# A recommender on one core: part of the history fetched as columns of an item table held in SBUF

## The chip, the core and the metric

The kernel runs on one core of a Trainium2 chip. The metric is the device time of one execution in microseconds (us). A core has five engines with queues of their own: PE (TensorE, matrix products), DVE (VectorE), ACT (ScalarE), POOL (GpSimd) and SP (SyncE, which here only issues transfers). On-chip memory is SBUF, with 128 partitions, and PSUM, which PE writes.

## The reference

There are 50,001 items and 16,384 users. An item has 32 neighbours. For two embeddings of 32 numbers (in and out) an attention of each item over its neighbours gives two vectors of 32. With a history embedding of 64 this makes an item row of 128; with a target embedding of 64, and the two vectors swapped, a target row of 128. Each user has a history of 100 items and one target.

```python
V = E[near_full]
scores = jnp.einsum('nd,nkd->nk', E, V) / jnp.sqrt(jnp.float32(GEO_HALF))
w = jax.nn.softmax(scores, axis=-1)
attn_of_item = jnp.einsum('nk,nkd->nd', w, V)
...
x = h * t[:, None, :]                      # h: [users, 100, 128], t: [users, 128]
z = jax.nn.relu(jnp.einsum('bld,hd->blh', x, W1) + b1)
scores = jnp.einsum('blh,h->bl', z, W2[0])
mask = (history != target[:, None]) & (history != 0)
exp_A = jnp.exp(scores) * mask
attn = exp_A / (jnp.sum(exp_A, axis=-1) ** 0.5)[:, None]
s = jnp.sum(h * attn[..., None])           # one number over everything
```

The result is the sigmoid of a cosine between the target row and a vector that has the number s in all places. So of each history row two things are needed: its score, and the plain sum of its 128 numbers. All data is float32.

## The kernel before

The kernel has two stages, one after the other, and a short end.

**Item stage.** Items go in 391 tiles of 128, each with 32 neighbours to fetch. POOL fetches most with one indirect gather of 128 rows per neighbour (line 238). The others come from `geoT`, the embedding table held transposed in SBUF: an item is a column there, and ACT and DVE copy one column of four bytes at a time (line 258), or PE copies it as a one-column product with the identity (line 253). A column's address stands in a register, and 32 registers are loaded at a time (line 197). SP fetches some neighbours row by row (line 226). The attention is worked out on DVE and ACT. `finish` (line 374) writes the rows to the tables `table` and `ttab` in DRAM.

**User stage.** Users go in 128 blocks of 128, and a block's 100 history positions in groups of 8 (the last of 4). For a group:

- `gather` (line 561) lets POOL fetch 8 rows per user with 8 indirect gathers (line 572), into one of six buffers.
- `turn` (line 581) transposes the 8 tiles on PE (line 587), multiplies them on DVE by the transposed target (line 589), and sums each row on DVE (line 592).
- `hidden` (line 601), one group later, multiplies by W1 on PE, 512 columns at a time (line 607), and applies Relu on ACT (line 608).
- `scored` (line 611), two groups later, multiplies each position by w2, a one-column product (line 616).

Each float32 product is two passes in the trace, a transpose one. `one_by_one` (line 534) has SP fetch some groups row by row, one transfer for each of 128 x 16 rows (line 555). `target_rows` and `target_work` fetch and transpose the target's rows, one gather per block (line 501). In the item stage the order of the engines' work is written out by hand; in the user stage it is the planner's, in the main over the loop at line 637.

Of the kernel before, what the change touches and what calls it, by code (L numbers as in the profile page):

```python
# [18 lines left out]
P = 128  # L19
ITEMS = 50001  # L20
K = 32
G = 32
# [32 lines left out]
BSUB = 4  # L55
LG = 4
NG = L // LG

UG = 2
UNIT = 42  # L60
AHEAD = 4
# [3 lines left out]
def kernel(  # L65
# [18 lines left out]
    geoT = nc.alloc_sbuf_tensor("geoT", (P, PAIRS), F32).ap()  # L84
# [3 lines left out]
    const = ctx.enter_context(tc.tile_pool(name="const", bufs=1))  # L88
    dram = ctx.enter_context(tc.tile_pool(name="dram", bufs=1, space=bass.MemoryType.DRAM))


    table = dram.tile([ROWS, D], F32, name="table")

    ttab = dram.tile([ROWS, D], F32, name="ttab")

    ident = const.tile([P, P], F32, name="ident")
    make_identity(nc, ident)
    ones = const.tile([P, P], F32, name="ones")
    nc.vector.memset(ones, 1.0)
    b1_sb = const.tile([HID, 1], F32, name="b1_sb")  # L100
    nc.sync.dma_start(b1_sb, b1.rearrange("(h o) -> h o", o=1))
    w2_sb = const.tile([HID, 1], F32, name="w2_sb")
    nc.sync.dma_start(w2_sb, w2.rearrange("o h -> h o"))
    w1_sb = const.tile([HID, D], F32, name="w1_sb")
    nc.sync.dma_start(w1_sb, w1)
    w1T = const.tile([D, HID], F32, name="w1T")
    with tc.tile_pool(name="wps", bufs=1, space=bass.MemoryType.PSUM) as wps:
        w1_ps = wps.tile([D, HID], F32, name="w1_ps")
        nc.tensor.transpose(w1_ps, w1_sb, ident)
        nc.vector.tensor_copy(w1T, w1_ps)  # L110
# [12 lines left out]
    with (  # L123
# [15 lines left out]
        def load(it):  # L139
# [5 lines left out]
            row = n_in.tile([P, NSUB, D + G], F32, name="row")  # L145
            nc.sync.dma_start(row[:, :, 0:DE], ehist_v[it])
# [216 lines left out]
        def attended(s):  # L363
            it, j = divmod(s, NSUB)
            row = its[it][2]
            att, tot = subs[s]["att"], subs[s]["ex"][1]
            nc.vector.tensor_tensor(
                row[:, j, DE:D].rearrange("p (t d) -> p t d", t=2),
                att,
                tot.to_broadcast([P, 2, G]),  # L370
                ALU.mult,
            )

        def finish(s):
            it, j = divmod(s, NSUB)
            row = its[it][2]
            nc.scalar.copy(row[:, j, D : D + G], row[:, j, DE : DE + G])

            if j == NSUB - 1 or (it == NITER - 1 and j == NSUB - 2):
                j0 = NSUB - 1 if it == NITER - 1 and j == NSUB - 1 else 0  # L380
                js = slice(j0, j + 1)
                nc.scalar.dma_start(ttab_v[it][:, js, DE:D], row[:, js, DE + G : D + G])
                nc.scalar.dma_start(table_v[it][:, js, :], row[:, js, 0:D])
# [75 lines left out]
    num = const.tile([P, UC], F32, name="num")  # L459
    den = const.tile([P, UC], F32, name="den")  # L460
    tsum = const.tile([P, UC], F32, name="tsum")
    tsq = const.tile([P, UC], F32, name="tsq")
    hist_v = history.rearrange("(p i j) l -> i p j l", p=P, j=BSUB)
    tidx = const.tile([P, UC], I32, name="tidx")
    nc.scalar.dma_start(tidx, target.rearrange("(p c) -> p c", p=P))
    tidf = const.tile([P, UC], F32, name="tidf")
    nc.vector.tensor_copy(tidf, tidx)
    with (
        tc.tile_pool(name="u_in", bufs=AHEAD + 2) as u_in,
        tc.tile_pool(name="u_t", bufs=2) as u_t,  # L470
        tc.tile_pool(name="u_h", bufs=6) as u_h,
        tc.tile_pool(name="u_hs", bufs=2) as u_hs,
        tc.tile_pool(name="u_x", bufs=2) as u_x,
        tc.tile_pool(name="u_s", bufs=2) as u_s,
        tc.tile_pool(name="ps_t", bufs=2, space=bass.MemoryType.PSUM) as ps_t,
        tc.tile_pool(name="ps_z", bufs=2, space=bass.MemoryType.PSUM) as ps_z,
        tc.tile_pool(name="ps_s", bufs=2, space=bass.MemoryType.PSUM) as ps_s,
    ):
        users = {}
        hists = {}  # L480
        LW = 2 * LG
        NW = -(-L // LW)
        in_order = mybir.DependencyInfo(
            mybir.DependencyClass.NoSync, mybir.DependencyReason.DATA
        )

        def width(g):
            return min(LW, L - g * LW)

        table_b = table.bitcast(U8).rearrange("(o r) d -> o (r d)", o=1)  # L490

        def history_of(i):
            hidx = u_in.tile([P, BSUB, L], I32, name="hidx")
            tc.keep_in_program_order(nc.sync.dma_start(hidx, hist_v[i]))
            hists[i] = hidx

        def target_rows(c):


            t = u_t.tile([P, D], F32, name="t")  # L500
            nc.gpsimd.indirect_dma_start(
                out=t,
                out_offset=None,
                in_=ttab[0:ITEMS, :],
                in_offset=bass.IndirectOffsetOnAxis(ap=tidx[:, c : c + 1], axis=0),
            )
            users[c] = {"t": t, "hidx": hists[c // BSUB][:, c % BSUB, :]}

        def target_work(c):
            u = users[c]  # L510
            t = u["t"]
            tT_ps = ps_t.tile([P, LG, P], F32, name="hT_ps")
            nc.tensor.transpose(tT_ps[:, 0, :], t, ident)
            tT = u_t.tile([D, 1, P], F32, name="tT")
            nc.vector.tensor_copy(tT[:, 0, :], tT_ps[:, 0, :])
            u["tT"] = tT
            nc.vector.tensor_reduce(tsum[:, c : c + 1], t, AX.X, ALU.add)
            junk = u_t.tile([P, D], F32, name="junk")
            nc.scalar.activation(junk, t, AF.Square, accum_out=tsq[:, c : c + 1])
            idf = u_s.tile([P, L], F32, name="idf")  # L520
            nc.scalar.copy(idf, u["hidx"])
            keep = u_s.tile([P, L], F32, name="keep")
            nc.vector.tensor_scalar(keep, idf, 0.0, None, ALU.not_equal)
            nc.vector.scalar_tensor_tensor(
                keep, idf, tidf[:, c : c + 1], keep, ALU.not_equal, ALU.mult
            )
            u["keep"] = keep
            u["hsum"] = u_s.tile([P, L], F32, name="hsum")
            u["score"] = ps_s.tile([P, L], F32, name="score")
            u["xT"], u["z"] = {}, {}  # L530

        early = {}

        def one_by_one(c, g):

            hs = u_hs.tile([P, UG * LW, D], F32, name="hs")

            hoff = u_hs.tile([P, UG * LW], I32, name="hoff")
            nc.vector.tensor_scalar(
                hoff,  # L540
                hists[c // BSUB][:, c % BSUB, g * LW : (g + UG) * LW],
                9,
                None,
                ALU.logical_shift_left,
            )
            for p in range(P):
                _, vals = nc.values_load_multi_w_load_instructions(
                    hoff[p : p + 1, :],
                    engines=[E.SP],
                    min_val=0,  # L550
                    max_val=(ITEMS - 1) * 4 * D,
                    skip_runtime_bounds_check_because="worked out from an item's number",
                )
                for q in range(UG * LW):
                    nc.sync.dma_start(
                        hs[p : p + 1, q, :].bitcast(U8), table_b[:, ds(vals[q], 4 * D)]
                    )
            for i in range(UG):
                early[c, g + i] = hs[:, i * LW : (i + 1) * LW, :]

        def gather(c, g):
            u = users[c]
            if (c, g) in early:
                u["h", g] = early.pop((c, g))
                u["got", g] = []
                return
            h = u_h.tile([P, LW, D], F32, name="h")
            u["got", g] = []
            for q in range(width(g)):
                l = g * LW + q  # L570
                u["got", g].append(
                    nc.gpsimd.indirect_dma_start(  # L572
                        out=h[:, q, :],
                        out_offset=None,
                        in_=table,
                        in_offset=bass.IndirectOffsetOnAxis(ap=u["hidx"][:, l : l + 1], axis=0),
                    )
                )
            u["h", g] = h

        def turn(c, g):
            u = users[c]
            w = width(g)
            h = u.pop(("h", g))
            hT_ps = ps_t.tile([P, LW, P], F32, name="hT_ps")
            for q in range(w):
                nc.tensor.transpose(hT_ps[:, q, :], h[:, q, :], ident)  # L587
            xT = u_x.tile([D, LW, P], F32, name="xT")
            x = nc.vector.tensor_tensor(  # L589
                xT[:, 0:w, :], hT_ps[:, 0:w, :], u["tT"].to_broadcast([D, w, P]), ALU.mult  # L590
            )
            s = nc.vector.tensor_reduce(  # L592
                u["hsum"][:, g * LW : g * LW + w], h[:, 0:w, :], AX.X, ALU.add
            )
# [147 lines left out]
```

## Time and profile before

| | us |
|---|---|
| median of three runs (29,659.82 to 29,660.97) | 29,659.96 |
| span of the profiled execution | 29,732.2 |
| POOL busy | 22,274.0 (75%) |
| PE busy | 20,868.1 (70%) |
| DVE busy | 14,649.3 (49%) |
| ACT busy | 10,176.0 (34%) |

The profile is of one execution, with its own time, a little longer than the median. Its lines give the source line, engine, operation and tiles (written from read), how often, the busy time, the mean duration of one in ns, and the idle time before them with what ended it. An idle time that ends with "issue" waited for nothing that the profile shows. Durations of one can overlap, so a pace is read from starts. The row PEclk gives the granted share of PE's clock in tenths, in 40 slices of the span; the other rows there are busy tenths. The clock is granted in windows of 3.41 us, at half or full rate in this trace.

### The profile page before, as it was taken

The page shows a single profiled execution, that of the slowest core. Times are in us where ns is not written, and L with a number is a line of the kernel's source. Part 1 is how long each engine was busy: PE and PEld are TensorE (multiplying, and loading weights), DVE is VectorE, ACT ScalarE, POOL GpSimd, SP SyncE. Part 2 cuts the span into 40 slices and gives each one's busy share as a digit, 9 for nine tenths or more (in the row PEclk, how much of TensorE's full clock was granted, in tenths as well). Part 3 has the DMA queues.
Part 4 walks back from the last instruction along what each step waited for, and adds up shares of the span by engine and source line. Part 5 has one row for each costly group of instructions (what it writes and reads, how often), then busy time and mean ns, then how long its engine had stood idle before and what let it go on. Part 6 is the DMA issues. An engine that isn't in the chain of part 4 may idle for free. (4 is left out here: it accounts for less than half of the span.)

```text
span 29732.2 us, 544828 instructions
## 1 busy us (share of the span) xinstructions
PE 20868.1 (70%) x85960; PEld 15598.5 (52%) x85960; DVE 14649.3 (49%) x92225; ACT 10176.0 (34%) x80592; POOL 22274.0 (75%) x23541
## 2 busy tenths in 40 slices
PE   5666666666666666667777777777777777777777
PEld 4666666666666666665444444444444444444444
DVE  5787777777877777774222222222222222222222
ACT  4555555555555555552111111111111111111111
POOL 7777777777777777777777777777777777777777
PEclk9999999999999999997666666666666666666666
DMA  3111111111111111112222222222222222222222
GB/s 68 34 33 33 35 34 32 33 35 34 33 33 35 34 33 33 35 33 47 53 54 54 54 54 54 54 54 54 54 54 54 54 54 54 54 54 54 54 54 52
DMA packets 1112201, 1351.31 MB, mean 45 GB/s; under 512 B 626480, under 2 KB 726256, under 8 KB 1108704
## 3 DMA queue, kind: packets, MB, share of 16 engines
q0 software_dynamic: 753120, 1186.89, 17.8%
q1 hardware_dynamic: 204528, 78.25, 1.0%
q10 hardware_dynamic: 151056, 51.31, 0.7%
q14 instruction: 2738, 22.43, 0.3%
q8 instruction: 759, 12.44, 0.2%
HBM read 1276.16 MB, written 51.30 MB: 45 GB/s over the span
## 5 line engine op out<-in xcount | busy, mean ns | idle before, releaser
L572 POOL DMA_INDIRECT h<-table,hidx x12512 | 11836.9, 946 | 3831.0 <-issue 3500.9
L238 POOL DMA_INDIRECT v<-in_egeo_dram,nidx x10895 | 10315.4, 947 | 3331.8 <-issue 3205.2
L253 PE MATMUL pc<-geoT,ident 128*128 x39424 | 8444.3, 352 | 312.5 <-issue 312.5
L253 PEld LDWEIGHTS pc<-geoT,ident 128*128 128x128 f32 x39424 | 8438.2, 333 | 392.9 <-issue 392.6
L258 ACT COPY g<-geoT 128x4 uint8 x73920 | 7265.1, 189 | 3174.6 <-issue 2704.0
L258 DVE COPY g<-geoT 128x4 uint8 x83776 | 6536.7, 196 | 1097.4 <-issue 1092.3
L589 DVE TENSOR_TENSOR xT<-hT_ps,tT 128x1024 f32<-128x1024 f32 (+1 forms) x1664 | 1969.0, 1183 | 10043.1 <-PE hT_ps L587 10043.1
L587 PE MATMUL hT_ps<-ident,h 128*128 128x128 f32 x12512 | 4502.9, 391 | 3162.9 <-DMA h<-table,hidx 3005.9
L608 ACT ACTIVATE z<-z_ps,b_sb 128x512 f32<-128x512 f32 x3200 | 2199.0, 687 | 11904.4 <-PE z_ps L607 11900.4
L587 PEld LDWEIGHTS hT_ps<-ident,h 128*128 128x128 f32 x12512 | 2177.1, 180 | 7692.6 <-DMA h<-table,hidx 6903.2
L607 PE MATMUL z_ps<-xT,w1T 128*128 128x512 f32 x6400 | 5585.9, 980 | 476.3 <-DVE xT L589 476.1
L616 PEld LDWEIGHTS score<-w_sb,z 128*128 128x128 f32 x25600 | 3759.7, 224 | 188.5 <-issue 167.7
L616 PE MATMUL score<-w_sb,z 128*128 128x1 f32 x25600 | 3494.9, 259 | 0.0
L281 PE MATMUL pt<-ident,g 128*128 128x128 f32 x1386 | 414.6, 435 | 4112.4 <-DVE g L258 3591.1
L281 PEld LDWEIGHTS pt<-ident,g 128*128 128x128 f32 x1386 | 270.5, 233 | 4185.4 <-issue 3220.7
L607 PEld LDWEIGHTS z_ps<-xT,w1T 128*128 128x128 f32 x6400 | 1810.9, 337 | 737.5 <-DVE xT L589 505.7
L592 DVE TENSOR_REDUCE hsum<-h 128x8 f32<-128x1024 f32 (+1 forms) x1628 | 1900.1, 1167 | 0.0
L307 DVE TENSOR_TENSOR prod<-v,own_ps 128x2048 f32<-128x2048 f32 x391 | 894.5, 2288 | 1340.0 <-DMA v<-in_egeo_dram 661.7
L347 DVE TENSOR_TENSOR wv<-v,ex 128x1024 f32<-128x1024 f32 x782 | 1473.8, 1886 | 0.0
L317 DVE TENSOR_REDUCE sc<-prod 128x64 f32<-128x2048 f32 x391 | 889.5, 2275 | 0.2
L360 DVE TENSOR_REDUCE att<-wv 128x64 f32<-128x2048 f32 x391 | 883.5, 2260 | 0.2
L289 ACT COPY v<-pt 128x256 f32<-128x256 f32 (+1 forms) x385 | 135.1, 351 | 1624.6 <-PE pt L281 1604.5
(74 smaller groups left out, 2045.9 us busy)
## 6 DMA issues: line engine op xcount, KB each, us to landing
hs<-table SPq DMA_DIRECT2D x36864, 0.5 KB
v<-in_egeo_dram SPq DMA_DIRECT2D x29568, 0.2 KB
h<-table,hidx POOLq DMA_INDIRECT x12512
v<-in_egeo_dram,nidx POOLq DMA_INDIRECT x10895
table<-row ACTq DMA_DIRECT2D x22, 1088.0 KB
own<-in_egeo_dram SPq DMA_DIRECT2D x23, 544.0 KB
row<-in_ehist_dram SPq DMA_DIRECT2D x23, 544.0 KB
ttab<-in_etgt_dram ACTq DMA_DIRECT2D x1, 12500.0 KB
```

What stands on the lines that cost most here:

```text
L238: nc.gpsimd.indirect_dma_start(out=v[:, k].rearrange("p t d -> p (t d)"), out_offset=None, in_=egeo, in_offset=bass.IndirectOffsetOnAxis(a ...
L253: nc.tensor.matmul(g[:, i : i + 1], ident, column.bitcast(F32), start=True, stop=True)
L258: copy(g.bitcast(U8)[:, 4 * i : 4 * i + 4], column)
L307: nc.vector.tensor_tensor(prod.rearrange("p k t d -> p k (t d)"), v.rearrange("p k t d -> p k (t d)"), subs[s]["own"].to_broadcast([P, K, ...
L347: nc.vector.tensor_tensor(subs[s]["wv"][:, t].rearrange("p d k -> p k d"), subs[s]["v"][:, :, t, :], subs[s]["ex"][0][:, t, :] .rearrange( ...
L572: nc.gpsimd.indirect_dma_start(out=h[:, q, :], out_offset=None, in_=table, in_offset=bass.IndirectOffsetOnAxis(ap=u["hidx"][:, l : l + 1], ...
L587: nc.tensor.transpose(hT_ps[:, q, :], h[:, q, :], ident)
L589: x = nc.vector.tensor_tensor(xT[:, 0:w, :], hT_ps[:, 0:w, :], u["tT"].to_broadcast([D, w, P]), ALU.mult)
L592: s = nc.vector.tensor_reduce(u["hsum"][:, g * LW : g * LW + w], h[:, 0:w, :], AX.X, ALU.add)
L607: nc.tensor.matmul(z_ps, w1T, xT[:, q : q + LG, :], start=True, stop=True)
L608: nc.scalar.activation(z[:, q : q + LG, :], z_ps, AF.Relu, bias=b1_sb)
L616: nc.tensor.matmul(u["score"][:, l : l + 1], z[:, q, :], w2_sb, start=True, stop=True)
```

## The change

The item stage stays, but for the row that it writes: `table` has rows of 129 numbers, the sum of the row first. The user stage is new.

- A stage between the two gives back `geoT`'s memory and loads the whole of `table` again, in 196 parts, to hold it transposed in SBUF as `tab` (128 x 50,001). The same loop fetches all target rows, 128 gathers, and stores them transposed in DRAM as `tgtT`.
- Of a block's 100 positions 88 are rows as before, in 30 groups of 3 (two of them of 2), in six row buffers of one tile each. SP fetches three rows in two blocks row by row, at the groups in `BY_SP`.
- The other 12 positions are six pairs. ACT copies the first of a pair, DVE the second, as 128 columns each out of `tab`, 25 or 26 in a group (`CHUNK`), over five groups a pair. The last nine of each (`EARLY`) are put off to the next group, ahead of its load of registers. The addresses are worked out once per block (`addresses`), in group 12 of the block before.
- PE takes a row's sum with a one-column product of the identity and the stored sum, and a pair's sums with a one-column product of the columns and a vector of ones.
- The order of all five engines is now written out by hand. In PE's: the sums of a pair if one is complete, the first row, the hidden product of the group before (and of a pair), the second row, the scores of the group two before (and of a pair), the third row.

```diff
+W = 1 + D
+GR = 3
+SIZES = ([3] * 14 + [2]) * 2
+NGR = len(SIZES)
+NROW = sum(SIZES)
+PAIRED = (L - NROW) // 2
+TURN = NGR // PAIRED
+CHUNK = (26, 26, 26, 25, 25)
+EARLY = 9
+BY_SP = (19, 39, 58)
+NRING = 6
+CH = 2
...
+                nc.vector.tensor_reduce(row[:, js, 0], row[:, js, 1:W], AX.X, ALU.add)
...
+    geoT_held.__exit__(None, None, None)
+    tc.strict_bb_all_engine_barrier()
+    tab_held = nc.sbuf_tensor("tab", (D, ITEMS), F32)
...
+            def turned(q):
...
+                nc.sync.dma_start(
+                    st[0:h, 0:n, :],
+                    table[base : base + h * n, 1:W].rearrange("(p n) d -> p n d", n=n),
+                )
+                ps = hidden_tile()
+                for r in range(n):
+                    nc.tensor.transpose(ps[:, r, 0:h], st[0:h, r, :], ident[0:h, 0:h])
+                into = tab[:, base : base + h * n].rearrange("d (p n) -> d n p", n=n)
+                copy = nc.vector.tensor_copy if q % 3 == 2 else nc.scalar.copy
+                copy(into, ps[:, 0:n, 0:h])
...
+            def addresses(c):
...
+                nc.tensor.transpose(cols_ps[0:n, :], colf[:, 0:n], ident)
+                nc.vector.tensor_copy(cols[r0:n, :], cols_ps[r0:n, :])
...
+            def turn(s, q):
+                c, g = divmod(s, NGR)
+                l = firsts[g] + q
+                h = rows[s][q]
+                nc.tensor.transpose(hT[s][:, q, :], h[:, 1:W], ident)
+                nc.tensor.matmul(sums[c][:, 1, l : l + 1], ident, h[:, 0:1], start=True, stop=True)
...
+            def columns(s, engine, of, early):
...
+                for i in range(n - EARLY, n) if early else range(n - EARLY):
+                    copy(
+                        into[:, 4 * (i0 + i) : 4 * (i0 + i) + 4],
+                        tab_b[:, ds(vals[i] - tab_at, 4)],
+                    )
...
+                if pairs[0]:
+                    pc, k = pairs[0]
+                    for i in range(2):
+                        l = NROW + 2 * k + i
+                        nc.tensor.matmul(
+                            sums[pc][:, 1, l : l + 1],
+                            pair[at[0] * TURN][:, i, :],
+                            unit,
+                            start=True,
+                            stop=True,
+                        )
+                for q in range(GR):
+                    if s < last and q < SIZES[g]:
+                        turn(s, q)
+                    if q == 0 and 1 <= s <= last:
+                        hidden(s - 1)
+                        relu(s - 1)
+                        if pairs[1]:
+                            x = pair[at[1] * TURN]
+                            zp = hidden_tile()[:, 0:2, :]
+                            nc.tensor.matmul(zp, w1T, x, start=True, stop=True)
+                            nc.scalar.activation(x, zp, AF.Relu, bias=b1_sb)
+                    if q == 1:
+                        if 2 <= s < last + 2:
+                            scored(s - 2)
+                        if pairs[2]:
+                            pc, k = pairs[2]
+                            for i in range(2):
+                                score(pc, NROW + 2 * k + i, pair[at[2] * TURN][:, i, :])
+                if s < last:
+                    times_target(s)
...
+                for engine, of in ((E.Activation, 0), (E.DVE, 1)):
+                    columns(s, engine, of, True)
+                    columns(s, engine, of, False)
```

## The prediction

> **What bounds the kernel now.** I read the page's slices first: they split the run into two stages.
>
> ```profile
> PE   5666666666666666667777777777777777777777
> ACT  4555555555555555552111111111111111111111
> POOL 7777777777777777777777777777777777777777
> PEclk9999999999999999997666666666666666666666
> L572 POOL DMA_INDIRECT h<-table,hidx x12512 | 11836.9, 946 | 3831.0 <-issue 3500.9
> ```
>
> POOL is level over both stages. Its 12,512 user gathers take (11,836.9 + 3,831.0) / 12,512 = 1.252 us each, and nearly all the idle time is the engine's own issuing: POOL bounds. One line's own view gives the stage's ends.
>
> ```profile
> L572 POOL DMA_INDIRECT h<-table,hidx x12512: 943/947/1038, 13673.8 to 29713.5; - x199
> ```
>
> The first target gather stands at 13,671 in the timeline, so the user stage is 29,732 - 13,671 = 16,061 us: 125.5 us for each of 128 user blocks. SP's rows come every 0.324 us beside it. PE is second, 11,986 us busy of 16,061, at a mean granted clock of 0.66. Since the change gives PE more work, I look at PE's pace in a stretch recorded at half clock (13,747 to 13,802 us), then in the item stage.
>
> ```profile
> 13749.18 1.91 PE L607 MATMUL z_ps<-xT,w1T 128*128 128x512 f32 x2
> 13750.89 0.93 PE L587 MATMUL hT_ps<-ident,h 128*128 128x128 f32 x2
> ...
> 13754.05 0.48 PE L587 MATMUL hT_ps<-ident,h 128*128 128x128 f32 x1 [0.32 <-DMA h<-table,hidx]
> 13754.32 1.71 PE L616 MATMUL score<-w_sb,z 128*128 128x1 f32 x8
> 13755.89 0.45 PE L587 MATMUL hT_ps<-ident,h 128*128 128x128 f32 x1
> ...
> 13576.81 27.46 PE L253 MATMUL pc<-geoT,ident 128*128 x128 [1.31 <-issue]
> ```
>
> Starts, not durations, give the pace. The hidden product of 512 columns takes 13750.89 - 13749.18 = 1.71 us (two passes), so 0.427 for a position of 128 columns. One-column products take 27.46 / 128 = 0.2145 us a pass, two passes each: 0.429. A transpose with eight such passes takes 13755.89 - 13754.05 = 1.84 us; less six passes (1.29), a transpose with one two-pass product is 0.55. All these halve at full clock (there a one-column pass takes 0.112 us). The clock row reads 9 in the item stage, but line 253 keeps the half-clock pace there, and the first gate record of the trace is at 13,693 us: those nines are no reading.
>
> When the gate opens is seen by cutting the stage at the gate's own 3.41 us windows, for the hidden products alone (columns: PE, weight loads, ACT, granted clock, DMA).
>
> ```profile
> 20004.11:20007.52 3.41, 0.25 (x1) 0.51 (x2) 0.00 (x0) 0.50 0.21 54
> 20007.52:20010.94 3.42, 2.79 (x4) 0.69 (x3) 0.69 (x1) 0.50 0.18 44
> 20010.94:20014.35 3.41, 0.46 (x1) 0.00 (x0) 0.69 (x1) 1.00 0.22 61
> 20014.35:20017.76 3.41, 0.38 (x1) 0.60 (x2) 0.00 (x0) 0.50 0.25 59
> 20017.76:20021.18 3.42, 2.94 (x4) 0.60 (x2) 0.69 (x1) 0.50 0.19 48
> 20021.18:20024.59 3.41, 0.32 (x1) 0.00 (x0) 0.69 (x1) 1.00 0.18 50
> ```
>
> A window at full clock follows one filled with hidden products: a group of 8 sends four passes in a row. I counted streaming time (transposes 0.213, hidden products by columns; one-column passes as nothing) in all 3,155 half-clock windows of the stage: under 2.4 us the next was never at full clock, over 2.7 always. Windows with 16 one-column passes closed the gate again.
>
> **The change, step by step.** *Item stage*: the row gains a sum (one DVE reduction per 17 tiles, near 2.3 us as line 360's) and 4 bytes; POOL still sets the pace. 13,671 us stay.
>
> *New stage between*: 196 loads of 128 KB turn the table, with 128 target gathers (128 x 1.25 = 160 us, beside it). Nearest row: the 66 loads of `st` between 55 and 181 us, 1.9 us each with three transposes, among other work. Bounds 200 us (1 us a load) and 450 us; SP's tgtT store waits each of 43 times for the step's end with the next loads behind it, so I take 350.
>
> *POOL, per user block*: 88 rows less 1.5 by SP = 86.5 x 1.252 = 108.3 us. Alone that is 17 us a block, 2,200 us in all, saved.
>
> *ACT*: 768 columns at 95 ns (32 in 3.14 us) are 73 us. Each of 30 loads of registers takes, scaled from 1.98 us for 32, 1.6 us for 25.6; the nine columns kept back hide 0.86, leaving 30 x 0.75 = 23. Thirty Relus near 0.52 (0.69 for 512) and the rest: 20. Sum 116 us. *DVE*: 768 x 0.071 + 30 x 1.15 + 30 x 0.58 + 4 = 110. *SP*: 192 x 0.324 + 6 x 2.2 = 75. All within 125.5. That line 592's reductions go (1,900 us of DVE) is worth nothing by itself: DVE was idle three quarters of the stage.
>
> *PE* at half clock: a row was 0.213 + 0.427 + 0.429 = 1.07 us, 107 us a block, inside 125.5. The row sum moves from DVE to PE: each row has one more one-column product with the identity as weights, two passes. A row is 0.55 + 0.427 + 0.429 = 1.41; 88 make 123.7. A position fetched as a column still needs sum, hidden product and score: 1.285 x 12 = 15.4. Together 139.1.
>
> PE also gains waits. (a) Once per five groups it sums a pair by column, first in the group's order, and waits for DVE's last nine columns, which DVE runs only after the product with the target: 0.25 (end of transpose) + 0.06 + 0.58 + 0.64 less the 0.43 that PE still has = 1.1 us, six times 6.6. (b) In group 12 the transpose of the addresses waits for a DVE queue of product, columns and five small operations: 0.2 + 0.58 + 3 + 0.9 less 0.3 = 4.4 us. Behind PE wait the transposes of rows already landed, and behind those the gathers, with six row buffers. Together 150.1 us a block, over POOL's 108: PE becomes the bound unless the gate opens.
>
> *Does it?* By the Trainium skill (TensorE: Matmul & The Clock Gate, Part 1) some 3.4 us of sustained matmul activity opens the gate and only idle closes it. PE without pauses would then be at full clock: 70 + 11 us, ACT the bound at 117 with its waits on PE, and the sum 13,671 + 350 + 128 x 117 + 20 = 29,017. The row of line 253 says otherwise: 27 us without a pause at half pace; streamed columns count, not weight loads. The groups of 3 now spread the hidden products: an ordinary window holds at most 3 x 0.213 + 1.28 = 1.92 us. Only a pair's group (0.85 more) can reach 3.23 us of dense work with 2.56 streamed, 2.7 with the next transpose, if the free-running window falls on it within a few tenths of a us. I allow one open window of six such groups: it does 6.8 us of half-clock work in 3.4. So 150.1 - 3.4 = 146.7 us a block. (The same page, Part 4, says that transposes don't count as busy; I count them, which favours the change.)
>
> *Sum*: 13,671 + 350 + 128 x 146.7 (18,778) + 20 for the end = 32,819 us in the profiled execution. The median of the runs is 29,660 to the profile's 29,732, 0.24% less: 32,740. I say 32,750, 10.4% slower.
>
> **Rivals.**
> - *The gate opens* (0.14, the other side): the place is PE's pace per block, the price 139 / (1 + share at full clock) + 11. With before's user stage plus the new one the break-even is (16,061 - 350) / 128 = 122.7 us, a share of 0.25; above it ACT's 117 soon binds, so 29,017, on the runs' scale 28,950. For: before had a share of 0.32 (clock 0.66). Against: it came from four passes in a row, which the change splits, and a gate opened here starves PE (six landed rows), so it closes again.
> - *The gate opens at times* (0.13): shares of 0.08 to 0.22 give 140 to 125 us, 30,000 to 31,900. For: a pair's group lies close to the threshold, and the period of five groups may lock to the window.
> - *The gate stays shut and more waits come* (0.05): each us a block is 128 us. Scores wait for ACT, a row of SP for its 128 transfers (near 50 us of the 100 there are). Over 33,900.
> - *POOL stays the bound and PE's work is hidden* (within the first): 108.3 a block would give 27,900; it needs ACT faster too.
>
> **How the numbers follow.** The main case has 0.68, its own range 32,100 (two open windows a block) to 33,250 (none, 150.1). To leave out no more than 2 in 10, the range goes down through most of the second rival and up past the new stage's bound: 30,800 to 34,000. Faster by over 0.2%, which is about what a measurement of this kernel can tell: 0.14. Within 0.2%: 0.02, where the share happens to be 0.25. Slower: 0.84.
>
> **What would show it.** Right: in the user stage POOL's idle time goes to waits for PE (the one-column sum that frees a row), PE is busy nearly throughout, the clock row near 0.5, rows every 1.6 us. PE's waits in that stage are for DVE's columns (six a block) and addresses (one, 4 us). Wrong: a clock row of 7 or more with POOL gathers still 1.25 us apart; or one-column passes with the identity under 0.2 us at half clock; or the new stage outside 200 to 450 us.

## The result, and the profile after

The changed kernel takes 39,965.43 us (median of four runs, 39,964.99 to 39,966.9) against 29,659.89 us before: 1.3475 times as long, with a 95% interval of 1.3456 to 1.3494. The forecast was 32,750 us, at most 34,000. The direction was right and the size was not.

First the slices of the changed kernel's page, which answer to the four rows shown of before.

```profile
PE   5666666666666577777777777777777777777777
ACT  4565565555555444444444444444444444444444
POOL 7777777777777544444444444444444444444443
PEclk9999999999999999555555555555555555555555
```

POOL is no longer level: in the user stage it falls from 7 to 4 tenths. The clock row settles at 5, as predicted. But PE, which was to be "busy nearly throughout", stands at 7, and ACT falls to 4. Nothing is full: something else is waited for.

The stage is cut into its parts next (the changed kernel; the columns are the length, then PE, weight loads, DVE, ACT and POOL busy, the granted clock, the DMA share and GB/s).

```profile
0.00:13650.00 13650.00, 8881.20 (x41030) 8703.85 (x41030) 10728.77 (x87867) 7862.11 (x76872) 10286.56 (x10901) 1.00 0.16 35
13650.00:14038.00 388.00, 149.98 (x517) 84.01 (x517) 104.87 (x274) 81.69 (x257) 120.67 (x128) 1.00 0.40 110
14038.00:39924.00 25886.00, 18560.79 (x71739) 15477.03 (x71740) 10091.51 (x104152) 11985.09 (x103189) 10436.36 (x11072) 0.54 0.12 30
```

The item stage ends at 13,650 us and the new stage takes 388. The whole loss lies in the user stage: 25,886 us from the first gather of history rows to the last, 202.2 us a block, where 125.5 were before and 146.7 forecast. PE is busy for 18,561 / 128 = 145.0 us of a block, so it waits 57.2.

Who waits for whom is in the changed kernel's waits (sum in us, times, longest) and in two of its groups.

```profile
POOL h L643 <- PE sums L656: 14370.7, 8391, 6.9
DVE pair L713 <- issue: 12321.8, 3888, 5.2
ACT pair L713 <- issue: 10150.6, 3835, 4.6
PE z L676 <- DVE xz L665: 4041.7, 1416, 4.5
...
PE sums L755 <- DVE pair L713: 1833.6, 767, 3.4
...
PE hT L604 <- DVE colf L601: 825.9, 128, 7.3
...
PE sums L755 <- ACT pair L713: 620.8, 646, 1.6
```

```profile
L643 POOL DMA_INDIRECT h<-table,hidx x11072 | 10437.3, 943 | 15449.7 <-PE sums L656 14370.7
L713 ACT COPY pair<-tab 128x4 uint8 x98304 | 10067.1, 190 | 10172.4 <-issue 10163.3
L713 DVE COPY pair<-tab 128x4 uint8 x98304 | 8100.6, 184 | 12349.0 <-issue 12337.0
```

POOL waits for the row sum that frees a row, as predicted (14,371 us). PE's four waits add up to 7,322 us, which is 57.2 us a block, all of what it isn't busy. All four are for what DVE or ACT owes. DVE and ACT in turn stand before their columns for 96 and 79 us a block "for issue": for nothing but their own queue. What the queue holds there is the load of registers, which isn't counted as busy. Its line shows it (minimum, median and maximum in ns): line 197 of the kernel before, which the forecast scaled from, then line 609 of the changed kernel.

```profile
L197 DVEq TENSOR_LOAD <-cols x2618: 2097/2152/6565, 221.2 to 13634.2; - x187
L197 ACTq TENSOR_LOAD <-cols x2310: 1937/1982/6642, 215.8 to 13626.7; - x193
```

```profile
L609 ACTq TENSOR_LOAD <-cols x3840: 1917/5372/5644, 14042.1 to 39939.3; - x192
L609 DVEq TENSOR_LOAD <-cols x3840: 2065/5589/5926, 14044.7 to 39942.5; - x192
L609 SPq TENSOR_LOAD <-cols x768: 2080/2174/2337, 14042.1 to 39844.7; - x192
```

A load of 25 or 26 registers takes 5.4 us at the median, where one of 32 took 1.98 before. The minimum of 1.92 says that some are still short. DVE's timeline in the changed kernel shows which:

```profile
20001.78 0.56 DVE L665 TENSOR_TENSOR xz<-hT,tT 128x384 f32<-128x384 f32 x1 [4.59 <-PE hT L655]
20002.25 0.86 DVE L713 COPY pair<-tab 128x4 uint8 x9
20007.76 1.24 DVE L713 COPY pair<-tab 128x4 uint8 x16 [4.65 <-issue]
20008.91 0.42 DVE L665 TENSOR_TENSOR xz<-hT,tT 128x256 f32<-128x256 f32 x1
...
20029.40 0.72 DVE L713 COPY pair<-tab 128x4 uint8 x9
20031.08 1.35 DVE L713 COPY pair<-tab 128x4 uint8 x17 [0.95 <-issue]
```

After the nine columns that were kept back comes the load, and then 16 or 17 columns. The gap is 4.65 us at one place and 0.95 at another. DVE's product with the target (line 665) stands behind it, PE's hidden product behind that, POOL's gather behind PE. Sorted by the five parts of `CHUNK`, the loads fall in two classes. `cols` holds four bytes a number:

| part | first byte | registers | ACT, us | DVE, us |
|---|---|---|---|---|
| 1 | 0 | 26 | 1.95 | 2.08 |
| 2 | 104 | 26 | 5.61 | 5.82 |
| 3 | 208 | 26 | 1.95 | 2.08 |
| 4 | 312 | 25 | 5.40 | 5.60 |
| 5 | 412 | 25 | 5.40 | 5.60 |

(Medians of 768 loads each; within a part they differ by at most 0.24 us.) The short ones start at a multiple of 16 bytes, the long ones don't, and those take 0.216 us a register on ACT. Three of five loads are long. (SP's loads of 32 all start at multiples of 128 bytes, and at 2.17 us they are as short as before.) The theory is that the start of the read, not the number of registers, is the cause. The rivals: PE's own work at half clock would have cost as much without the long loads; or a load is long for where it stands between columns, not for its address.

### The profile page after: what moved, and what is told of

Same layout as the page of the kernel before. It is cut to its first block, busy times and chain, and to the rows that moved or that the text cites. A ratio compares the mean times of both kernels' runs of the same rounds, so it can differ in the third digit from the quotient of the medians.

```text
span 39964.1 us, 799690 instructions
## 1 busy us (share of the span) xinstructions
PE 27610.5 (69%) x113357; PEld 24280.8 (61%) x113357; DVE 20940.0 (52%) x192415; ACT 19945.1 (50%) x180432; POOL 20844.5 (52%) x22101
## 5 line engine op out<-in xcount | busy, mean ns | idle before, releaser
L713 ACT COPY pair<-tab 128x4 uint8 x98304 | 10067.1, 190 | 10172.4 <-issue 10163.3
L713 DVE COPY pair<-tab 128x4 uint8 x98304 | 8100.6, 184 | 12349.0 <-issue 12337.0
L676 PE MATMUL z<-xz,w1T 128*128 128x384 f32 (+1 forms) x7680 | 6178.6, 908 | 4047.9 <-DVE xz L665 4047.9
L656 PEld LDWEIGHTS sums<-h,ident 128*128 128x128 f32 x22144 | 6162.8, 344 | 1355.1 <-issue 1355.0
L685 PE MATMUL sums<-small,xz 128*128 128x1 f32 x22528 | 5293.0, 350 | 0.0
L685 PEld LDWEIGHTS sums<-small,xz 128*128 128x128 f32 x22528 | 5218.7, 330 | 0.2
L655 PE MATMUL hT<-ident,h 128*128 128x128 f32 x11072 | 4874.2, 440 | 1.8 <-DMA h<-table,hidx 1.8
L656 PE MATMUL sums<-h,ident 128*128 128x1 f32 x22144 | 4686.9, 281 | 0.0
L655 PEld LDWEIGHTS hT<-ident,h 128*128 128x128 f32 x11072 | 3515.2, 317 | 952.0 <-issue 854.8
L680 ACT ACTIVATE xz<-z,small 128x384 f32<-128x384 f32 (+1 forms) x3840 | 2182.7, 568 | 3738.5 <-PE z L676 3696.6
```

What stands on the lines that cost most here:

```text
L655: nc.tensor.transpose(hT[s][:, q, :], h[:, 1:W], ident)
L656: nc.tensor.matmul(sums[c][:, 1, l : l + 1], ident, h[:, 0:1], start=True, stop=True)
L676: nc.tensor.matmul(z[s][:, 0:w, :], w1T, xz[s][:, 0:w, :], start=True, stop=True)
L680: nc.scalar.activation(xz[s][:, 0:w, :], z.pop(s)[:, 0:w, :], AF.Relu, bias=b1_sb)
L685: nc.tensor.matmul(sums[c][:, 0, l : l + 1], of, w2_sb, start=True, stop=True)
L713: copy(into[:, 4 * (i0 + i) : 4 * (i0 + i) + 4], tab_b[:, ds(vals[i] - tab_at, 4)],)
```

## Experiments

The first three ran on another chip, where the kernel before takes 49,331.25 us, so from them only durations, the user stage's length and ratios among themselves are carried over. The same kernel (e1 and e4) begins its user stage at 24,833 us there and at 14,062 on the other; why isn't known.

**e1: the same columns, reads that start at multiples of 16 bytes.** A load begins up to three numbers earlier and throws those away.

```diff
+                    at0 = i0 // 4 * 4
                     live[engine] = registers(
-                        c, 2 * k + of, engine, i0, n, tab_at, tab_at + 4 * (ITEMS - 1)
-                    )
+                        c, 2 * k + of, engine, at0, i0 + n - at0, tab_at, tab_at + 4 * (ITEMS - 1)
+                    )[i0 - at0 :]
```

> Only the place where a read of registers begins is changed: it is rounded down to a multiple of four numbers (16 bytes) in the row of addresses, up to three registers more are read, and the same columns are fetched in the same groups. Theory 1 (alignment): the reads that took 5.4 to 5.8 us begin 104, 312 and 412 bytes into the row, those of 1.94 us at 0 and 208; so all reads take 1.9 to 2.1 us here, PE at half clock becomes the bound with 147 to 152 us a block, and the time is 32,900 to 33,500 us. Theory 2 (the number of registers, 25 or 26 not being a multiple of four, or contention of the two engines): three reads in five stay over 5 us and the time stays within 2% of 39,965. Rival to the clock's part: freed of the waits, PE opens its clock gate, and the time is 29,000 to 29,500.

Measured: 45,621.62 us, 0.9247 of before on that chip (0.9232 to 0.9263). ACT's loads fall to a median of 1.937 us and DVE's to 2.070, with no long ones left. The user stage takes 20,744 us, 162.1 a block, and PE is busy for 89% of it. That speaks for the address, since every load stayed in its place; but the long ones now also read two or three numbers more, and only e3 changes the address alone. The pace that was expected, 147 to 152 us a block, was missed (e4 shows what was left out). The ratio below 1 says nothing of the kernel on the first chip: there the question was put again, as e4.

**e2: e1 with the row sums copied by DVE.** This takes 88 two-pass products with the identity off PE in each block, and puts a one-column copy for each on DVE.

```diff
-                nc.tensor.matmul(sums[c][:, 1, l : l + 1], ident, h[:, 0:1], start=True, stop=True)
...
+                for q in range(w):
+                    l = firsts[g] + q
+                    nc.vector.tensor_copy(sums[c][:, 1, l : l + 1], rows[s][q][:, 0:1])
```

> Besides the aligned reads, the sum of a row goes from PE (a one-column product of two passes) to DVE (a copy of one number per partition). If PE at half clock is the bound with aligned reads, PE loses 88 x 0.34 = 30 us a block and keeps 109 plus waits of some 12: 118 to 124 us a block, 29,200 to 29,900 us. If something else is the bound there, the time is that of the aligned kernel, within 2%, or longer by DVE's 88 x 0.1 = 9 us a block (1,100 us).

Measured: 45,438.43 us, 0.921 of before (0.9194 to 0.9225); 20,540 us of user stage, 160.5 a block. PE's busy time fell from 143.6 to 117.6 us a block, but the time hardly moved: 118 to 124 us a block were expected if PE set the pace, so this is a miss. The waits of this kernel say where it went.

```profile
POOL h L643 <- DVE sums L669: 4708.8, 2651, 6.8
...
POOL h L643 <- DVE pair L787: 2499.1, 728, 13.8
...
PE sums L758 <- DVE sums L669: 962.0, 550, 4.8
...
PE z L678 <- DVE xz L661: 889.9, 1112, 3.4
...
PE hT L655 <- DMA h<-table,hidx: 101.7, 158, 3.0
```

A row is now freed by DVE, after its product for the whole group, and the gathers wait for DVE in place of PE. But that isn't what costs the time: PE waits only 0.8 us a block for a row to land (101.7 / 128). PE's waits are 42.8 us a block in all, where 18.1 were in e1: 18.9 before a pair's sums (line 758; 11.7 in e1), 16.9 before the hidden product (line 678; 2.0 in e1) and 5.6 before the addresses. The row sums that left PE had, it seems, filled the time in which DVE works out the product, and on DVE they stand in front of other work for which PE waits. So a lighter PE isn't enough by itself.

**e3: the kernel before, with the item stage's addresses eight bytes later.** Nothing else is touched; each of its loads of 32 registers there starts at byte 8 of 16.

```diff
-            cols = n_in.tile([n, P], I32, name="cols")
+            cols = n_in.tile([n, P + 4], I32, name="cols")[:, 2 : P + 2]
```

> The kernel before, with nothing changed but that the rows of addresses in the item stage begin 8 bytes later in memory. Theory 1 (alignment): each read of 32 registers takes 32 x 0.216 = 6.9 us in place of 1.98, on ACT, DVE, PE and SP; ACT with six reads for a tile then needs 6 x 6.0 + 192 x 0.095 + 3 = 57 us in place of the 34.9 that POOL sets, so the item stage grows from 13,670 to about 22,000 us and the whole to about 38,000. Theory 2 (number of registers): nothing changes, 29,660.

Measured, in one run: 58,804.47 us against 49,331.25 for the kernel before on the same chip. The loads of this kernel:

```profile
L197 DVEq TENSOR_LOAD <-cols x2618: 7122/7337/12169, 361.9 to 33776.8; - x187
L197 ACTq TENSOR_LOAD <-cols x2310: 6797/6908/11771, 365.5 to 33771.3; - x193
```

32 registers at 0.216 us are 6.91 us, and 6.908 was measured on ACT, 3.5 times the 1.982 of the aligned read. The address is thus the cause, and no affair of the new stage or its order: eight bytes of shift bring the long loads into the kernel before.

**e4: e1 once more, on a chip like the first.** The edit is e1's.

> The kernel with aligned reads once more, since the chip of the first run of it was one on which the kernel before too took 49,331 us. If the cause was the chip alone, and PE at half clock is the bound of the user stage: 14,040 us up to the user stage and 150 to 162 us a block, 33,200 to 34,800 us, beside 29,660 for the kernel before. If the chip is again the slow one, the user stage alone is compared: 20,700 us as in the first run.

Measured: 34,446.39 us, 1.1611 of before (1.1592 to 1.1631), before being 29,661.36. Long loads are therefore worth 39,965 - 34,446 = 5,519 us of the 10,306 lost. The other 4,785 stay, and they are what the forecast was about. The aligned kernel's user stage in one row, and the waits of PE in it:

```profile
14062.00:34425.00 20363.00, 18402.74 (x71742) 15403.10 (x71743) 10531.48 (x104157) 12281.77 (x103207) 10465.73 (x11072) 0.52 0.18 39
```

```profile
POOL h L643 <- PE sums L656: 8843.3, 8251, 12.9
...
PE sums L756 <- ACT pair L714: 605.4, 63, 12.3
PE sums L756 <- DVE pair L714: 599.0, 704, 1.1
...
PE hT L604 <- DVE colf L601: 562.6, 128, 4.8
...
PE z L676 <- DVE xz L665: 142.5, 219, 1.2
```

20,363 / 128 = 159.1 us a block: 143.8 of PE's work and 15.3 of waits, of which these four make 14.9. The largest wasn't foreseen: 63 waits of up to 12.3 us for ACT's columns. ACT's timeline in this kernel has the reason.

```profile
14395.43 1.62 ACT L714 COPY pair<-tab 128x4 uint8 x16 [0.42 <-issue]
14407.16 0.33 ACTq L734 DMA_DIRECT2D tT<-tgtT  x1
14408.05 0.34 ACTq L511 DMA_DIRECT2D hidx<-in_history_dram  x1
14409.02 0.33 ACTq L512 DMA_DIRECT2D hidx<-in_target_dram  x1
14409.46 0.58 ACT L680 ACTIVATE xz<-z,small 128x384 f32<-128x384 f32 x1 [12.41 <-DMA tT<-tgtT]
```

In every second block, 63 times, ACT's transfer of the next target (line 734) starts some 10 us after ACT's queue reaches it. The trace records the semaphore (a counter on which one engine waits for another) that each transfer waits for. SP's transfers of a row use eight of them in turn, and ACT's transfers use the same ones. In all 63 stalls the transfer starts 0.02 us after a transfer of SP's has landed that counts on the very semaphore it waits for; so it stands behind transfers of a row that SP has yet to send. In the blocks between, SP's last landing on that semaphore lies 23 us or more back when ACT arrives; in the changed kernel, whose blocks are longer, it lies at least 5.7 us back, though in every second block SP is amid a row there too, and nothing is held.

**e5: five pairs, aligned, with DVE copying the row sums.** 90 rows and ten columns; a pair's columns over six groups, the parts of `CHUNK` multiples of four. The copies of a group's first two sums stand before DVE's product with the target and the last after it, and PE takes a pair's sums and turns the addresses later in its order.

```diff
-SIZES = ([3] * 14 + [2]) * 2
+SIZES = [3] * 30
-CHUNK = (26, 26, 26, 25, 25)
+CHUNK = (24, 20, 20, 24, 20, 20)
...
+                row_sums(s, range(w - 1))
                 nc.vector.tensor_tensor(
...
+                row_sums(s, range(w - 1, w))
```

> Aligned reads; row sums copied by DVE, two of three ahead of the product with the target; the sums of a pair and the transpose of the addresses at places in PE's order where what they need is ready; five pairs (10 positions as columns) in place of six. If PE at half clock and its waits were what bound the aligned kernel: PE has 90 x 1.07 + 10 x 1.285 = 109 us a block, POOL 88.5 x 1.252 = 111, DVE about 103, ACT 94; with 111 to 118 us a block the time is 28,300 to 29,200 us, faster than the kernel before. If six row buffers bound it (rows are freed by DVE now, and a gather takes near 3 us from issue to use): 125 to 140 us a block, 30,000 to 32,000.

Measured: 31,331.75 us, 1.0563 of before (1.0545 to 1.0581), 134.7 us a block. That lies in the second range, for which six row buffers were to be the bound. PE is busy 14,933 / 128 = 116.7 us of it. The kernel's waits:

```profile
POOL h L646 <- DVE sums L664: 3951.2, 3544, 4.7
DVE sums L664 <- PE sums L695: 3051.5, 2460, 5.0
...
PE z L686 <- DVE xz L671: 1635.6, 2985, 1.7
...
PE z L686 <- DVE sums L664: 378.9, 630, 1.1
...
PE hT L658 <- DMA h<-table,hidx: 43.7, 87, 1.1
```

The number was met, its cause wasn't: POOL waits for DVE to free rows, but PE waits for a row to land only 87 times, 0.3 us a block. What PE waits for is DVE: of 18.1 us a block, 15.8 stand before the hidden product (line 686). At the median DVE's product starts 0.11 us after the last transpose that it reads, and PE's hidden product 0.06 us after the product ends; between the two PE has one transpose to do and then stands for 0.51 us, in each of 30 groups. DVE's copies also wait 23.8 us a block for PE's scores, with which they share nothing but the PSUM tile `sums`; since the product follows the last transpose so closely, this can cost little. So PE's work and this handing over between PE and DVE set the pace. That is read from the trace and wasn't tested.

**e6: the same with six pairs.** Only `SIZES` and `CHUNK` go back to what the changed kernel has.

```diff
-SIZES = [3] * 30
-CHUNK = (24, 20, 20, 24, 20, 20)
+SIZES = ([3] * 14 + [2]) * 2
+CHUNK = (26, 26, 26, 25, 25)
```

> As the kernel with five pairs, but with six (12 positions as columns, 88 as rows). POOL 108 us a block, PE 110, DVE 113 to 118, ACT 105. If DVE and ACT set the pace rather than the row buffers, this is slower than five pairs by 2 to 7 us a block (250 to 900 us); if the row buffers do, it is faster by the two rows less (2 to 3 us a block).

Measured: 31,827.73 us, 1.073 of before (1.0712 to 1.0748), 138.6 us a block. Against e4, which has the same rows and columns, this is 20.5 us a block less, with 26.5 us less of work on PE (143.8 to 117.3). So PE's work at half clock did set e4's pace in large part. Its waits make up the rest: before a pair's sums and the addresses they fall from 9.4 + 4.4 us a block to nothing, but before the hidden product they rise from 1.1 to 18.1.

```profile
PE z L686 <- DVE xz L671: 1849.9, 2800, 2.5
...
PE hT L658 <- DMA h<-table,hidx: 14.9, 26, 1.6
```

Against e2, which also has the row sums on DVE but all after the product, it is 22 us less (e1 and e4, one kernel on the two chips, differ by 3). PE has the same work in both, and the waits before a pair's sums and the addresses, 18.9 + 5.6 us a block in e2, are gone: the order of the work counts for as much as its amount. Six pairs take 1.6% more than five, 3.9 us a block. That is the case expected if DVE and ACT set the pace rather than the row buffers, and it agrees with PE's waits in e5; so here more columns don't pay.

No version was found that beats the kernel before. With the new stage in it, the user stage would have to come below the 122.7 us a block of the forecast's break-even. Whether e5 comes there when PE has other work to do before each hidden product, or when the sums have a tile of PSUM of their own, wasn't tried.

## Why the prediction was wrong in size

*The step that failed* is ACT's and DVE's share of a block: "Each of 30 loads of registers takes, scaled from 1.98 us for 32, 1.6 us for 25.6". It scaled a duration by the count and carried over, unsaid, that the new reads start where the old ones did. They don't: 26 + 26 + ... of four bytes start at 104, 312 and 412. Measured, two loads of five took 1.95 us and three 5.4 to 5.6. For ACT that is 18 loads a block at some 3.5 us more, 63 us; DVE is alike. "All within 125.5" fell with it: ACT's busy time and its waits for issue make 93.6 + 79.3 = 173 us, DVE's 78.8 + 96.3 = 175, and with what these two wait for PE, and PE for them, 202.2.

With that one fact put right, the sums for both engines hold nearly. In e4 ACT has 95.9 + 19.0 = 114.9 us a block (forecast 116) and DVE 82.3 + 33.4 = 115.6 (forecast 110). The new stage took 388 us (350, between bounds of 200 and 450) and the item stage stayed.

*PE as the bound* was right in kind, and so the direction wasn't luck: in e4 DVE and ACT wait 42.6 and 37.1 us a block for PE. But it was sized too low as well, and e4's 34,446 us too lie above the range. e4 has 159.1 us a block against 146.7, and the 12.4 between are:

- PE's work, 143.8 against 139.1 less 3.4 for an open window: 8.1 us, from the hidden product and the gate. The row sum was sized well: a transpose, 0.213 us without it, takes 0.53 with it (forecast 0.55). The hidden product wasn't: with 384 columns the second pass starts 0.80 us after the first, where 0.427 us for 128 columns in two passes give 0.64, and some 30 of those are 4.7 us.
- The gate. It stays shut, as argued from the row of line 253, even though PE is 90% busy in e4; the rule of the Trainium skill (TensorE: Matmul & The Clock Gate, Part 1), that some 3.4 us of sustained matmul activity open it, would have put the changed kernel at 29,017 us by the forecast's working. But the one open window a block was too many: in the part of each trace that has gate records, there are 75 windows at full clock in some 119 blocks of the changed kernel, and 52 in some 125 of e4.
- PE's waits, 15.3 against 11: 4.3 us. Wait (b), for the addresses, was forecast at 4.4 us a block and is 562.6 / 128 = 4.4 in e4. Wait (a), for DVE's columns, was 6.6 and is 4.7. ACT's held transfer brings another 4.7, and the hidden product's wait for DVE 1.1.

*The rivals.* The gate did not open, and POOL did not stay the bound. The case that came true was the one with a chance of 0.05, "the gate stays shut and more waits come", but by none of the mechanisms named for it (scores, SP's rows): the loads of registers stood in the sum as a settled figure. It was an open term and called for a bound, but the trace of before held no price for it: all of ACT's and DVE's reads there start at multiples of 128 bytes. Its maximum of 6,642 ns beside a median of 1,982 is no sign of the effect. 22 of ACT's 2,310 loads take over 5 us there, with the same starts as the others; why isn't known. What could be seen beforehand is only that the new reads start elsewhere.

*Slips that decided nothing.* By its own terms the main case's range is 32,300 to 33,170 us, not 32,100 to 33,250. And the trace of before has 3,239 half-clock windows with one behind them, not 3,155; the two bounds on streaming come out the same (none of 1,903 windows under 2.4 us is followed by one at full clock, all of 1,160 over 2.7 are).

## What to carry to other kernels

When a kernel takes addresses from SBUF into registers in parts, start each part at a multiple of 16 bytes and make its length a multiple of four numbers; reading a few too many is cheaper than reading them one by one. Scale a measured duration to a new size only after asking what else of the operation changes with the size, its start address among it. And before taking work off the engine that sets the pace, see what it will wait for instead: in e2 the 26 us a block saved on PE came back as waits, most of them for DVE, and only with the work placed anew (e6) did part of them count. An engine that waits for buffers, as POOL does here, isn't the bound while nobody waits for what it delivers.

## What the hardware showed that was not expected

A load of registers seems to go by fours where it can. ACT's medians over all runs: 20 registers 1.26 us, 24 1.50, 28 1.74, 32 1.98, which is 0.24 to 0.25 us per four. 26 take 1.95 and 27 take 2.16: six fours and two or three single ones at 0.216 us. Reading 28 is thus quicker than reading 26. From a start that isn't a multiple of 16 bytes every register takes as long as a single one: 25 take 5.40, 26 5.61, 32 6.91. DVE's are alike (5.60, 5.82 and 7.34). The profile counts none of it as busy time: it appears only as idle time "for issue" in front of the instruction that uses the registers.
